# Mixing the expert weights of the last taps and of the third convolution on VectorE, from a layout by experts

## The chip, the core and the metric

The kernel runs on one core of one Trainium2 chip. The metric is the device time of one execution in microseconds (us). TensorE is written PE, VectorE DVE, ScalarE ACT, GpSimd POOL, SyncE SP; PEld is PE's loading of weights.

## The reference, cut to what matters

The program computes four layers on x of 4 images, 512 channels, 64x64, all in fp32. The change lies in layer 1, a conditional convolution: each image has its own weights, mixed from eight experts.

```python
def _L1_conv_ref(x, router_w, router_b, w1, w2, w3, g1, b1, m1, v1, ...):
    def _cond_conv(x, experts, rw, stride, padding):
        W = jnp.einsum('be,eoihw->boihw', rw, experts)          # one weight per image
        ...                                                      # convolution of each image with its W
    pooled = x.mean(axis=(2, 3))
    rw = jax.nn.sigmoid(pooled @ router_w.T + router_b)          # 8 numbers per image
    out = _cond_conv(x, w1, rw, 1, 0)                            # 1x1, 512 -> 128
    out = jax.nn.relu(_bn(out, g1, b1, m1, v1))
    out = _cond_conv(out, w2, rw, 1, 1)                          # 3x3, 128 -> 128
    out = jax.nn.relu(_bn(out, g2, b2, m2, v2))
    out = _cond_conv(out, w3, rw, 1, 0)                          # 1x1, 128 -> 512
    out = _bn(out, g3, b3, m3, v3)
    return jax.nn.relu(out + x)
```

Layer 0 is an attention over the 4096 positions with head size 64, layer 2 a linear attention with softplus features, layer 3 a projection with discounted cumulative sums along rows and columns and a gate.

## The kernel before

The images are worked through one after the other; for each of them `layer0` to `layer3` run in this order, and `xs` holds the image as four tiles of 128 partitions x 4 x 1024 ("pairs" of two blocks of 512 positions). PE's order is the order of the program over the whole kernel (`manual_schedule` with PE). DVE's order is the program's in the blocks of code that say so (the tail of `layer0`, the start of `layer2` and two parts after it, `layer3`). Elsewhere a scheduler places the instructions of DVE, ACT, POOL and SP.

**The weights of layer 1** are 17 pieces of 128 x 128: pieces 0 to 3 are the first convolution (`conv1`, one piece per 128 input channels), 4 to 12 the nine taps of the second, 13 to 16 the third (`conv3`). The mixed pieces stand in `wc`, the first 17 slices of the tile `wcq`. Each image loads the experts anew in five loads by SP: `ex0` (pieces 0-3), `ex4` (4-6), `ex7` (7-9), `ex10` (10-12), `ex13` (13-16). They go into buffers that are free at the time: `ex4`, `ex10`, `ex13` in the pool `bigp` (three buffers), `ex7` in `xpool`, `ex0` in `wlate`.

**Mixing on PE (`mix`, L170).** The DRAM tensor `packed` has on each partition one of four experts and one of 32 input channels: partition (e, i), then piece, quarter q of the input channels, half g of the experts, output channel. `sel` is 128 x 2 x 32: rw of the expert where the partition's i is the column's i, else zero. A matmul with `sel[:, g, :]` as weights sums four experts for 32 input channels; eight matmuls (two g, four q, each q in its own 32 columns of the array) give n pieces in one PSUM bank, and ACT copies them into `wc` (L178).

**Around it.** At the end of `layer0` (from L352, DVE in the program's order) the last pair's attention is normalised, rw is formed on DVE (L363 to L366), and from it `own` (L368), `part` (L371) and `sel` (L374). PE's order there is: two products of the output projection (`y`, L291), logit, another `y`, `mix` of `ex0`, the last `y`; then in `layer1` `mix` of `ex4` and `ex7`, `conv1(0)`, `mix` of `ex10`, `conv1(1)`, `conv1(2)`, `mix` of `ex13`, `conv1(3)`. After that comes `layer2`, which starts with the second and third convolutions: `conv2(0)`, `conv2(1)`, `conv3(0)`, `conv2(2)`, `conv3(1)` and so on.

The second convolution works on six sums of shifted rows instead of the rows themselves: `sums_of_six(pr)` (L430) forms them on DVE from `conv1`'s output of pair `pr`, twelve instructions of 128 x 256; `sums_of_taps` (L402) forms the matching sums of the nine taps on ACT and DVE, so it needs pieces 4 to 12 mixed. `conv2(pr)` (L459) has 36 matmuls less those at the edge; then ACT copies half of the result to `sp` (L472), DVE combines (`dq`, L473, to L480), ACT applies batch norm and relu (L484). `conv3` (L489) has two matmuls for each of four output blocks, and DVE adds the image (L495). In `layer2` DVE's order is written as `sums_of_six(0)`, `(1)`, `(2)`, the end of `conv2(0)`, `sums_of_six(3)`, the end of `conv2(1)`, the end of `conv3(0)`.

The PSUM tag `s` has three buffers of two banks (products `y`, `conv1`, `conv2`, `conv3` take them in turn), the tag `acc` two of one bank (`mix`, and the edge sums of `conv2`).

Of the kernel before, what the change touches and what calls it, by code (L numbers as in the profile page):

```python
# [8 lines left out]
F32 = mybir.dt.float32  # L9
AF = mybir.ActivationFunctionType  # L10
ALU = mybir.AluOpType
# [4 lines left out]
P = 128  # L16
# [4 lines left out]
KC = C // P  # L21
# [4 lines left out]
E = 8  # L26
# [19 lines left out]
def unshifted(ctx: ExitStack, tc: tile.TileContext, fits, x, wqkv_t, wout_t, router_t,  # L46
# [3 lines left out]
    nc = tc.nc  # L50
# [3 lines left out]
    bigp = ctx.enter_context(tc.tile_pool(name="bigp", bufs=3))  # L54
# [8 lines left out]
    def bank(name, shape=(P, NB)):  # L63
        return ps.tile(list(shape), F32, tag="acc", name=name)
# [16 lines left out]
    def load_pair(b, pr):  # L81

        t = xpool.tile([P, KC, 2 * NB], F32, tag="x", name=f"x_{b}_{pr}")
        src = x[b, :, pr * 2 * NB:(pr + 1) * 2 * NB].rearrange("(kc p) n -> p kc n", p=P)
        if b == 0 and pr == 0:
            for kc in range(KC):
                nc.sync.dma_start(t[:, kc, :], src[:, kc, :])
        else:
            nc.sync.dma_start(t, src)
        return t  # L90
# [4 lines left out]
    xs = [load_pair(0, pr) for pr in range(NPAIR)]  # L95
# [66 lines left out]
                             start=kc == 0, stop=kc == KC - 1)  # L162
        nc.vector.tensor_scalar(wr_sb, wo_t[:, 1, 0:E], col(SCALE), 1.0 / HW, ALU.mult, ALU.mult)

    def load_experts(b, j, n, pool, tag):
        ex = pool.tile([P, n, 4, 2, P], F32, tag=tag, name=f"ex_{b}_{j}")
        nc.sync.dma_start(ex, packed[:, j:j + n])
        return b, j, n, ex

    def mix(wc, sel, experts):  # L170

        b, j, n, ex = experts
        y = bank(f"mix_{b}_{j}", (P, n, P))
        for g in range(2):
            for q in range(4):
                nc.tensor.matmul(y[32 * q:32 * (q + 1)], sel[:, g, :], ex[:, :, q, g, :], start=g == 0, stop=g == 1,  # L176
                                 tile_position=(0, 32 * q))
        nc.scalar.copy(wc[:, j:j + n, :], y)  # L178

    def layer0(b, xs):  # L180


        tc.keep_in_program_order(nc.scalar.preload_act_table_set("natural_log_exp_and_others"))
        ex0 = load_experts(b, 0, KC, wlate, "late")
        key = bigp.tile([P, HW], F32, tag="big", name=f"key_{b}")
        qv = bigp.tile([P, 2, NPAIR * NB], F32, tag="big", name=f"qv_{b}")
# [95 lines left out]
        def sum_range(pr):  # L282
            i = b * NPAIR + pr
            nc.vector.tensor_reduce(stat[:, 0, i:i + 1], recs[pr], AX.X, ALU.add)
            nc.vector.tensor_reduce(stat[:, 1, i:i + 1], recs[pr], AX.X, ALU.min)
# [58 lines left out]

        pr = NPAIR - 1
        ex4 = load_experts(b, 4, 3, bigp, "big")
        for i in groups[-1]:
            values(i)
        ex7 = load_experts(b, 7, 3, xpool, "x")
        wcq = bigp.tile([P, NPIECE + 1 + 4 * NPAIR, P], F32, tag="big", name=f"wc_{b}")  # L350
        ex10 = load_experts(b, 10, 3, bigp, "big")
        with tc.manual_schedule(engines={mybir.EngineType.DVE}):  # L352
            sums(pr, early=False)
            for m in range(KC):
# [7 lines left out]
            rw = small.tile([P, E], F32, tag="rw", name=f"rw_{b}")  # L362
# [9 lines left out]
            sel = small.tile([P, 2, 32], F32, tag="sel", name=f"sel_{b}", bufs=1)  # L372
# [9 lines left out]
                xm = xs[pr - 1][:, m, :]  # L382
                nc.vector.tensor_tensor(xm, xm, flat(ring[8 + m]), ALU.add)
            sum_range(pr)
        return wcq, sel, ex4, ex7, ex10

    def layer1(b, xs, wcq, sel, ex4, ex7, ex10):
        wc = wcq[:, 0:NPIECE, :]
        qs = wcq[:, NPIECE + 1:, :].rearrange("p (a j) c -> p a (j c)", a=NPAIR)

        mix(wc, sel, ex4)
        mix(wc, sel, ex7)

# [6 lines left out]
        def sums_of_taps():  # L402
            part = block(f"part_{b}", (P, 4, P))[:, 0:3, :]
            nc.scalar.activation(taps[:, 0], g0, AF.Copy, scale=0.25)
            for k, c0, c1 in ((1, -1 / 6, 1 / 6), (3, 1 / 24, -1 / 12)):
                c2 = -1 / 6 if k == 1 else 1 / 6
                nc.scalar.activation(part, g0, AF.Copy, scale=c0)
                nc.vector.scalar_tensor_tensor(part, g2, c2, part, ALU.mult, ALU.add)
                nc.vector.scalar_tensor_tensor(taps[:, k], g1, -c1, part, ALU.mult, ALU.add)
                nc.vector.scalar_tensor_tensor(taps[:, k + 1], g1, c1, part, ALU.mult, ALU.add)  # L410
# [6 lines left out]
        def conv1(pr):  # L417
            y = pair_psum(f"c1_{b}_{pr}")
            for h in range(2):
                for kc in range(KC):  # L420
                    nc.tensor.matmul(y[:, h, :], wc[:, kc, :], xs[pr][:, kc, h * NB:(h + 1) * NB],  # L421
                                     start=kc == 0, stop=kc == KC - 1)
            rows = h1[:, :, 2 * pr * ROWS:2 * (pr + 1) * ROWS, :]
            yq = y.rearrange("p h (r q f) -> p f (h r) q", q=W // 4, f=4)
            for f in range(4):
                q = 1 if f == 0 else 0
                nc.scalar.activation(rows[:, f, :, q:q + W // 4], yq[:, (f - 1) % 4], AF.Relu,
                                     bias=bn_t[:, 0:1], scale=bn_s[:, 0:1])
# [67 lines left out]
                nc.scalar.activation(xm, xm, AF.Relu, bias=bn_t[:, 2 + m:3 + m])  # L496

        conv1(0)
        mix(wc, sel, ex10)
        sums_of_taps()  # L500
        conv1(1)
        ex13 = load_experts(b, 13, KC, bigp, "big")
        conv1(2)
        mix(wc, sel, ex13)
        conv1(3)
        return sums_of_six, conv2, conv3, wcq, qs

    def layer2(b, xs, sums_of_six, conv2, conv3, wcq, qs):

        ks = small.tile([P, NPAIR], F32, tag="ks", name=f"ks_{b}")  # L510
        g = bank(f"g_{b}", (P, C))
# [78 lines left out]
        with tc.manual_schedule(engines={mybir.EngineType.DVE}):  # L590
            sums_of_six(0)
            sums_of_six(1)
            sums_of_six(2)
            h2 = {0: conv2(0)}
            sums_of_six(3)
            h2[1] = conv2(1)
            conv3(0, h2[0])
# [288 lines left out]
    with tc.manual_schedule(engines={mybir.EngineType.PE}):  # L886
        for b in range(B):
            convs = layer1(b, xs, *layer0(b, xs))
            xs = layer3(b, xs, *layer2(b, xs, *convs))
# [395 lines left out]
@with_exitstack  # L1285
def tile_kernel(ctx: ExitStack, tc: tile.TileContext, *args):
    nc = tc.nc
    flagp = ctx.enter_context(tc.tile_pool(name="flagp", bufs=1))
    fits = flagp.tile([1, 2], mybir.dt.int32, tag="fits", name="fits")
    unshifted(tc, fits, *args)  # L1290

    n = nc.values_load(fits[0:1, 0:1], min_val=0, max_val=P)
    with tc.If(n < P):
        general(tc, *args)
# [50 lines left out]
```

## Time and profile before

| | |
|---|---|
| median of 3 runs | 2735.74 us (2735.30 to 2735.93) |
| the profiled execution's own time | 2737.18 us |
| its span, first to last instruction | 2735.4 us |
| mean granted PE clock | 0.998 |
| PE busy, share of the span | 2682.8 us, 98% |
| DVE busy | 1918.6 us, 70% |
| ACT busy | 1310.5 us, 48% |
| `mix` on PE, 12 mixes of three pieces (128x384) | 17.1 us in 192 records |
| `mix` on PE, 8 mixes of four pieces (128x512) | 15.4 us in 128 records |
| ACT's copies of mixed weights (L178) | 20, of 0.48 us (384) or 0.59 us (512) |
| loads of experts by SP | 12 of 1536 KB, 6.1 us to landing; 8 of 2048 KB, 7.6 us |

A page's line of a group gives the line of the kernel, the engine, the operation, out<-in by name and shape, the number of instructions, their busy time, the mean duration of one in ns, and the idle time of the engine just ahead of them with what ended it. In the chain of waits each row is a start, a duration and what ran; the chain is followed back from the last instruction to whatever released it. In the timeline each row is a start, a duration, the engine, and in brackets the idle time before it. PE's records show each fp32 matmul as two.

### The profile page before, as it was taken

Reading aid. Unit: us, or ns where it says so; the run is one execution under the profiler, and the core shown is the slowest. Engines: PE = TensorE matmul, PEld = TensorE weight load, DVE = VectorE, ACT = ScalarE, POOL = GpSimd, SP = SyncE. Lnnn points to the kernel's source line nnn. Section 1 sums busy time; section 2 is a strip of 40 time slices with the busy share of each in tenths; the row PEclk is TensorE's granted clock in tenths of the full one; section 3 lists DMA queues with packets and bytes.
Section 4 is the critical chain, followed back from the end, with each engine's and each line's share of the span. In section 5 each row is a group of like instructions: output and inputs, shape, how many; then the busy total and the mean of one; then the engine's idle time right before and its main releaser. Section 6 shows DMA issues by size and latency. Waiting matters only on the chain.

```text
span 2735.4 us, 25841 instructions
## 1 busy us (share of the span) xinstructions
PE 2682.8 (98%) x10174; PEld 1116.4 (41%) x10174; DVE 1918.6 (70%) x2133; ACT 1310.5 (48%) x1491; POOL 10.7 (0%) x26
## 2 busy tenths in 40 slices
PE   8999999999999999999999999999999999999998
PEld 3333364344333345444433334544443333454443
DVE  2688656787478766678747776667874787666787
ACT  4545344445554535345555553535554545352545
POOL 1000000000000000000000000000000000000000
PEclk9999999999999999999999999999999999999999
DMA  5000210021200021002220002101121000210011
GB/s 187 1 1 0 100 31 1 16 108 76 78 0 1 1 101 31 0 23 100 77 77 1 1 1 100 31 1 55 69 107 47 1 1 10 92 31 0 31 44 50
DMA packets 31986, 115.17 MB, mean 42 GB/s; under 512 B 2928, under 2 KB 12144, under 8 KB 29296
## 3 DMA queue, kind: packets, MB, share of 16 engines
q1 hardware_dynamic: 31856, 113.43, 11.0%
q8 instruction: 82, 1.34, 0.2%
q14 instruction: 48, 0.39, 0.0%
HBM read 79.86 MB, written 33.55 MB: 41 GB/s over the span
## 4 chain that ended last, share of the span: by engine, by line
PE 87%; DVE 8%; ACT 2%; issue 1%; DMA 1%; SPq 1%; DVEq 0%; ACTq 0%
PE s L237 17%; PE av L252 16%; PE sx L747 14%; PE zy L747 11%; PE kq L198 4%; PE c L421 4%; PE c L470 3%; PE c L493 2%; PE z L522 2%; PE vv L198 2%; PE wv L665 2%; PE g L584 2%; PE xtr L567 2%; PE y L291 2%; PE c2e L470 2%; PE mix L176 1%
## 5 line engine op out<-in xcount | busy, mean ns | idle before, releaser
L237 PE MATMUL s<-qv,key 64*128 64x512 f32 x2048 | 468.2, 602 | 1.8 <-ACT ring L240 1.8
L245 DVE TENSOR_TENSOR acc<-acc,ring 128x1024 f32<-128x1024 f32 x312 | 381.7, 1223 | 100.8 <-ACT ring L240 71.6
L240 ACT ACTIVATE ring<-s 128x1024 f32<-128x1024 f32 x336 | 317.7, 1039 | 223.6 <-PE s L237 223.6
L252 PE MATMUL av<-ring,qv 128*64 128x512 f32 x1344 | 304.5, 595 | 0.0
L237 PEld LDWEIGHTS s<-qv,key 64*128 64x128 f32 x2048 | 188.9, 187 | 274.3 <-issue 171.8
L245 DVE TENSOR_TENSOR acc<-acc,ringx 128x1024 f32<-128x1024 f32 x168 | 205.5, 1223 | 101.0 <-ACT ringx L240 88.2
L240 ACT ACTIVATE ringx<-s 128x1024 f32<-128x1024 f32 x176 | 172.1, 1040 | 206.0 <-PE s L237 206.0
L747 PE MATMUL sx<-t,sx 128*128 128x512 f32 x512 | 236.9, 597 | 0.0
L252 PEld LDWEIGHTS av<-ring,qv 128*64 128x64 f32 x1344 | 93.3, 137 | 198.6 <-issue 198.6
L252 PE MATMUL av<-ringx,qv 128*64 128x512 f32 x704 | 167.2, 598 | 0.0
L752 ACT COPY zy<-sx 128x512 f32<-128x512 f32 x64 | 36.5, 570 | 240.1 <-PE sx L747 230.6
L797 DVE TENSOR_TENSOR_SCAN t<-sx,t 128x512 f32<-128x512 f32 x128 | 148.8, 1210 | 1.7
L747 PEld LDWEIGHTS sx<-t,sx 128*128 128x128 f32 x512 | 95.9, 190 | 127.8 <-issue 121.1
L786 ACT COPY t<-s 128x1024 f32<-128x1024 f32 x64 | 127.1, 1993 | 40.5 <-DVE s L780 40.5
L756 ACT ACTIVATE e<-sx,prm_sb 128x512 f32<-128x512 f32 x128 | 87.0, 687 | 123.8 <-PE sx L747 123.8
L780 DVE TENSOR_TENSOR_SCAN s<-wc,s 128x512 f32<-128x512 f32 x128 | 146.0, 1204 | 0.0
L803 ACT ACTIVATE s<-t 128x1024 f32<-128x1024 f32 x64 | 125.5, 1987 | 1.0 <-DVE t L797 0.9
L747 PE MATMUL sx<-t,wq 128*128 128x512 f32 x256 | 117.0, 598 | 7.5 <-ACT e L756 7.5
L198 PE MATMUL kq<-x,wqkv_sb 128*64 128x512 f32 x512 | 117.0, 610 | 6.0 <-DMA x<-in_x_dram 6.0
L747 PE MATMUL zy<-t,wq 128*128 128x512 f32 x256 | 118.7, 604 | 2.5 <-ACT zy L752 2.5
L747 PE MATMUL zy<-x,wq 128*128 128x512 f32 x256 | 116.2, 594 | 0.0
L747 PE MATMUL sx<-x,wq 128*128 128x512 f32 x256 | 116.2, 594 | 0.0
(193 smaller groups left out, 3368.4 us busy)
## 6 DMA issues: line engine op xcount, KB each, us to landing
out_dram<-s SPq DMA_DIRECT2D x64, 512.0 KB, 2.6
x<-in_x_dram SPq DMA_DIRECT2D x15, 2048.0 KB, 8.3
ex<-in_packed_dram SPq DMA_DIRECT2D x12, 1536.0 KB, 6.1
ex<-in_packed_dram SPq DMA_DIRECT2D x8, 2048.0 KB, 7.6
wq<-in_wproj_t_dram SPq DMA_DIRECT2D x32, 256.0 KB, 5.1
x<-in_x_dram SPq DMA_DIRECT2D x4, 512.0 KB, 6.6
wv_sb<-in_wv_t_dram SPq DMA_DIRECT2D x1, 1024.0 KB, 11.4
wqkv_sb<-in_wqkv_t_dram SPq DMA_DIRECT2D x1, 384.0 KB, 3.1
```

Of the source, the lines that this page charges most:

```text
L198: nc.tensor.matmul(y[h * D:(h + 1) * D, :], wqkv_sb[:, kc, col0:col0 + D], xs[pr][:, kc, h * NB:(h + 1) * NB], start=kc == 0, stop=kc == K ...
L237: nc.tensor.matmul(s[:, h, :], key[r, kt * P:(kt + 1) * P], qry[r, pr * NB:(pr + 1) * NB], start=True, stop=True)
L240: nc.scalar.activation(p, s, AF.Exp)
L245: nc.vector.tensor_tensor(accs[pr], accs[pr], p, ALU.add)
L252: nc.tensor.matmul(avs[pr][h * D:(h + 1) * D, :], vt[:, kt, :], ring[i % RING][:, h, :], start=kt == 0, stop=kt == NT - 1)
L421: nc.tensor.matmul(y[:, h, :], wc[:, kc, :], xs[pr][:, kc, h * NB:(h + 1) * NB], start=kc == 0, stop=kc == KC - 1)
L470: nc.tensor.matmul(y[:, lo - a:hi - a], u, v[:, lo:hi], start=dy == 1, stop=dy == 2)
L747: nc.tensor.matmul(y, w[:, c, self.kind, self.j * P:(self.j + 1) * P], v[:, c, :], start=c == 0 and k in (1, 5), stop=c == 1, skip_group_c ...
L780: nc.vector.tensor_tensor_scan(self.half(i, h), along[:, self.j + 2 * i, :], self.half(i, h), 0.0, ALU.mult, ALU.add)
L786: nc.scalar.copy(self.t[i].rearrange("p (w r) -> p w r", w=W), self.s[i].rearrange("p (r w) -> p w r", w=W))
L797: nc.vector.tensor_tensor_scan(th, down[:, i, :], th, 0.0, ALU.mult, ALU.add)
L803: nc.scalar.activation(self.s[i].rearrange("p (r w) -> p w r", w=W), tw, AF.Sigmoid)
```

## The change

Two of the five mixes, of `ex10` (the last three taps) and of `ex13` (the third convolution), are done on DVE. Their experts are loaded from the DRAM tensor `experts`, which has for each piece and input channel (a partition) the eight experts' 128 outputs one after the other; so a partition's data of one piece is a run of 4 KB, where `packed` had one run of 12 or 16 KB for all pieces of the load. `mix_by_expert` multiplies the first expert's slice by rw's first column, and adds the seven others with a multiply and add each. rw is handed on to `layer1`. The mix of `ex10` is written at the start of `layer1`, that of `ex13` in `layer2` after `sums_of_six(2)`, ahead of `conv2(0)`. The three mixes of pieces 0 to 9 stay as they were.

```diff
--- before.py
+++ after.py
@@ -162,10 +162,21 @@
                              start=kc == 0, stop=kc == KC - 1)
         nc.vector.tensor_scalar(wr_sb, wo_t[:, 1, 0:E], col(SCALE), 1.0 / HW, ALU.mult, ALU.mult)
 
-    def load_experts(b, j, n, pool, tag):
-        ex = pool.tile([P, n, 4, 2, P], F32, tag=tag, name=f"ex_{b}_{j}")
-        nc.sync.dma_start(ex, packed[:, j:j + n])
+    def load_experts(b, j, n, pool, tag, pack=True):
+        if pack:
+            ex = pool.tile([P, n, 4, 2, P], F32, tag=tag, name=f"ex_{b}_{j}")
+            nc.sync.dma_start(ex, packed[:, j:j + n])
+        else:
+            ex = pool.tile([P, n, E, P], F32, tag=tag, name=f"ex_{b}_{j}")
+            nc.sync.dma_start(ex, experts[j:j + n].rearrange("n p e c -> p n e c"))
         return b, j, n, ex
+
+    def mix_by_expert(wc, rw, experts):
+        _, j, n, ex = experts
+        to = wc[:, j:j + n, :]
+        nc.vector.tensor_scalar(to, ex[:, :, 0, :], rw[:, 0:1], None, ALU.mult)
+        for e in range(1, E):
+            nc.vector.scalar_tensor_tensor(to, ex[:, :, e, :], rw[:, e:e + 1], to, ALU.mult, ALU.add)
 
     def mix(wc, sel, experts):
 
@@ -348,7 +359,7 @@
             values(i)
         ex7 = load_experts(b, 7, 3, xpool, "x")
         wcq = bigp.tile([P, NPIECE + 1 + 4 * NPAIR, P], F32, tag="big", name=f"wc_{b}")
-        ex10 = load_experts(b, 10, 3, bigp, "big")
+        ex10 = load_experts(b, 10, 3, bigp, "big", pack=False)
         with tc.manual_schedule(engines={mybir.EngineType.DVE}):
             sums(pr, early=False)
             for m in range(KC):
@@ -382,14 +393,15 @@
                 xm = xs[pr - 1][:, m, :]
                 nc.vector.tensor_tensor(xm, xm, flat(ring[8 + m]), ALU.add)
             sum_range(pr)
-        return wcq, sel, ex4, ex7, ex10
-
-    def layer1(b, xs, wcq, sel, ex4, ex7, ex10):
+        return wcq, sel, rw, ex4, ex7, ex10
+
+    def layer1(b, xs, wcq, sel, rw, ex4, ex7, ex10):
         wc = wcq[:, 0:NPIECE, :]
         qs = wcq[:, NPIECE + 1:, :].rearrange("p (a j) c -> p a (j c)", a=NPAIR)
 
         mix(wc, sel, ex4)
         mix(wc, sel, ex7)
+        mix_by_expert(wc, rw, ex10)
 
 
 
@@ -496,16 +508,14 @@
                 nc.scalar.activation(xm, xm, AF.Relu, bias=bn_t[:, 2 + m:3 + m])
 
         conv1(0)
-        mix(wc, sel, ex10)
         sums_of_taps()
         conv1(1)
-        ex13 = load_experts(b, 13, KC, bigp, "big")
+        ex13 = load_experts(b, 13, KC, bigp, "big", pack=False)
         conv1(2)
-        mix(wc, sel, ex13)
         conv1(3)
-        return sums_of_six, conv2, conv3, wcq, qs
-
-    def layer2(b, xs, sums_of_six, conv2, conv3, wcq, qs):
+        return sums_of_six, lambda: mix_by_expert(wc, rw, ex13), conv2, conv3, wcq, qs
+
+    def layer2(b, xs, sums_of_six, mix_last, conv2, conv3, wcq, qs):
 
         ks = small.tile([P, NPAIR], F32, tag="ks", name=f"ks_{b}")
         g = bank(f"g_{b}", (P, C))
@@ -591,6 +601,7 @@
             sums_of_six(0)
             sums_of_six(1)
             sums_of_six(2)
+            mix_last()
             h2 = {0: conv2(0)}
             sums_of_six(3)
             h2[1] = conv2(1)
```

## The prediction

> **What bounds the kernel now.** I read the busy shares first, then the shares of the chain that ended last, then that chain in order of time over one image's tail of layer 0 and layer 1 (300 to 362 us, first image), then VectorE (DVE) over the same stretch. From the page:
>
> ```profile
> PE 2682.8 (98%) x10174; PEld 1116.4 (41%) x10174; DVE 1918.6 (70%) x2133; ACT 1310.5 (48%) x1491; POOL 10.7 (0%) x26
> ...
> PE 87%; DVE 8%; ACT 2%; issue 1%; DMA 1%; SPq 1%; DVEq 0%; ACTq 0%
> ```
>
> TensorE (PE) is busy for 98% of the span and holds 87% of the chain: what leaves PE's queue is time, and so is what makes PE wait. The chain in order of time (start, us, what):
>
> ```profile
> 306.53 0.18 DVE own L368
> ...
> 306.73 0.17 DVE part L371
> ...
> 306.93 0.25 DVE sel L374
> ...
> 307.22 1.92 PE mix L176 x16
> 309.14 1.06 PE y L291 x4
> 310.20 2.72 PE mix L176 x32
> 312.92 7.07 PE c L421 x16
> 319.99 1.43 PE mix L176 x16
> 321.41 13.93 PE c L421 x32
> 335.34 1.85 PE mix L176 x16
> 337.20 7.07 PE c L421 x16
> 344.26 5.07 PE c L470 x24
> ```
>
> Three readings. The mixing of pieces 10-12 (319.99) and 13-16 (335.34) stands on the chain with conv1 (L421) before and after it. Two conv1 without a mix between them (321.41) take 13.93 us. And own, part, sel lie on the chain just before PE's first mix: PE stands still there. DVE over the stretch (start, us, ..., idle before it and who ended it):
>
> ```profile
> 317.12 0.68 DVE L285 TENSOR_REDUCE stat<-rec 128x1 f32<-128x512 f32 x1
> 321.99 0.76 DVE L440 SCALAR_TENSOR_TENSOR t<-h 128x256 f32<-128x256 f32 x2 [4.19 <-ACT h L427]
> ...
> 341.53 0.42 DVE L440 SCALAR_TENSOR_TENSOR wl<-t,t 128x256 f32<-128x256 f32 x1
> 349.99 0.69 DVE L473 TENSOR_TENSOR dq<-c,sp 128x512 f32<-128x512 f32 x1 [8.04 <-ACT sp L472]
> ```
>
> DVE has two holes here, 4.19 and 8.04 us; the other images show 4.18, 4.18, 3.60 and 8.04 each.
>
> [...] L533 takes 691 ns at N=1024, L726 with two tensors 1222. [...] the trace has no load of experts in 4 KB runs, only loads of x in such runs (2048 KB in 8.3 us, against 7.6 for experts of the same size in 16 KB runs).
>
> **The change, part by part.** The instruction order of both kernels, compared engine by engine, differs only in what follows.
>
> *PE, removed.* Two mixes of eight matmuls per image. A further conv1 in a row costs 13.93 - 7.07 = 6.86 us, and the last one 344.26 - 337.20 = 7.06 up to conv2. From the first conv1 to conv2 it was 344.26 - 312.92 = 31.34; without mixes it is 3 x 6.86 + 7.06 = 27.64. **Saved: 3.70 us per image, 14.8 in four** (the other images have the same distances to 0.01 us). ACT loses two copies (0.48 and 0.58 us), off the chain.
>
> *DVE, added.* Eight dependent instructions per mix. The nearest rows:
>
> ```profile
> L533 DVE TENSOR_SCALAR sp<-sp 128x1024 f32<-128x1024 f32 x16 | 11.1, 691 | 52.3 <-ACT sp L532 52.3
> ...
> L409 DVE SCALAR_TENSOR_TENSOR wl<-wc,part 128x384 f32<-128x384 f32 x8 | 4.4, 552 | 0.0
> ...
> L656 DVE SCALAR_TENSOR_TENSOR kv<-bv_sb,ksum,gk 128x512 f32<-128x512 f32 x4 | 3.0, 748 | 1.0 <-PE gk L655 1.0
> ```
>
> A scalar read per partition costs some 60 ns more (L808 750 against L769 689). So a step is 0.61 us at 384 elements and 0.75 at 512. The first multiply[...] is an estimate of 0.36 + 0.06 = 0.42 and 0.42 + 0.06 = 0.48 (0.61 and 0.75 if not). A dependent instruction starts 0.03 us after the end of the one that it reads (L448 at 338.14, after 337.35 + 0.76). Mix of 10-12: 0.42 + 0.03 + 7 x 0.64 = 4.9 us. Mix of 13-16: 0.48 + 0.03 + 7 x 0.78 = 6.0 us. Together 11 us an image, 44 on DVE; what matters is where.
>
> *In front of sel.* The scheduler put the first two steps of the mix of 10-12 ahead of sel: the multiply between own and part, the first add between part and sel. PE's mix of 0-3 waits for sel, and all of PE's queue behind it. With the multiply at 306.73, the add starts at 306.73 + 0.42 + 0.03 = 307.18, and sel, not dependent on it, some 0.08 before its end (four L296 of 1.28 us take 4.85), at 307.71 in place of 306.93: 0.78. If the multiply needn't wait for own (0.1 earlier), 0.68. I take **0.75 us per image, 3.0 in four**. Bounds: 0.55 (no surcharge for the scalar) and 1.0[...]; never a gain[...].
>
> *The wait that comes with it.* The multiply waits for the load of pieces 10-12. Behind it stand part, sel and four L296, and so PE. In SP's queue this load is second of three: issued at 294.76, 6.1 us to landing, thus at 300.9, 5.8 us before DVE asks. Its 128 packets of 12 KB become 384 of 4 KB: I take 0.1 to 0.6 us more ([...]8.3 against 7.6 scaled to 1.5 MB). The next load (pieces 7-9, landed at 305.5, used after 311) may come as much later. Cost nothing, covered by 5 us.
>
> *The other six steps of 10-12* come after L285: 6 x 0.64 = 3.8 us, in the 4.19 hole. L285 ends at 317.8 + 0.75, the steps at 322.4. The hole's end moves with conv1 to 321.99 + 0.75 = 322.7. Fits by 0.3 us; the last image, with its hole of 3.60, misses by 0.3, which the next hole (2.26 us before 337.35, about 1.3 after the change) takes up.
>
> *Load of 13-16.* SP now waits for DVE's last step (322.4) rather than PE's mix (issued at 321.5 before). Landing 7.6 us later, at 330; DVE asks at 341. Behind it in SP's queue are only the projection's weights, at 388.8. Nothing.
>
> *mix_last*, 6.0 us, goes into the 8.04 hole. conv1 now starts at 312.92 + 0.75 = 313.67 and conv2 at 341.3, 2.95 earlier. The sums of six of the third pair follow the third conv1: it ended at 321.41 + 13.93 = 335.3 and will end at 313.67 + 3 x 6.86 = 334.25, so those sums end 1.0 earlier, at 340.9, and mix_last at 346.9. L473 could start 2.95 earlier, at 347.0. **It fits with next to nothing to spare.** Behind it is some cover: conv3's fourth product needs the PSUM buffer that the first L495 frees. Before, that was freed at 362.97 and wanted at 364.6, so about 1.6 us of overflow cost nothing. Pieces 13-16 are first wanted by conv3, 10 us later still.
>
> *Sum.* 14.8 - 3.0 = 11.8 us. Against the profiled execution's own 2737.2 (span 2735.4, 1.8 around it) that is 2725.4; against the median of the runs shown, 2735.74, 1.4 lower, **2724.0**. Layers 2 and 3 and the next image's loads are released by PE's and DVE's progress, and the images follow each other at an even 677 us, so nothing swallows the shift. Some 0.2%, 5.5 us, is what a measurement of this kernel can tell from no change.
>
> **Rivals.**
> 1. *DVE overflows.* If a step took 1.2 us (the slices of the experts reading slower than rows), mix_last would take 9.6, overflow 3.5, pay 3.5 - 1.6 = 1.9; before sel the delay would be about 1.5: gain 3.7 - 3.4 = 0.3 an image, about 2734.5. For it: a fit with no reserve. [...]
> 2. *The load is late and DVE stands before sel*: the change ends **slower**. The place is the multiply between own and part. It costs PE one for one once the load takes more than 306.7 - 294.8 = 11.9 us, eats the gain at 11.9 + 2.95 = 14.9 us, and is slower by 0.2% past 16.2. At three times the present time to landing, 18.3 us: 6.4 - 2.95 = 3.45 an image lost, 2749.5. For it: a new layout with three times the packets. Against it: loads of x with such packets bring 2 MB in 8.3 us.
> 3. *Sel isn't held up.* If the two steps cost PE nothing, 14.8 us are gained: 2721. Against it: sel is on the chain.
> That the change doesn't do what it says is excluded: the order shows 16 matmuls per image gone from PE and 16 DVE instructions added.
>
> **How the numbers follow.** Forecast (sel's delay 0.55 to 1.0: 2723.1 to 2725.0; with an overflow of mix_last paid by up to 1 us an image, to 2729): 0.80. Rival 3: 0.04. Rival 1 and milder forms that leave under 5.5 us: 0.10. Rival 2: 0.06. So faster 0.84, same 0.10, slower 0.06. Range 2720.5 to 2731.
>
> **What would show it.** Right: no mix between conv1s, conv1 to conv2 in 27.6 us; DVE's multiply after own without a wait for a DMA; PE's wait before the first mix longer by 0.7; L473 still waiting for ACT's sp, or for mix_last by tenths. Wrong: a DMA as the releaser of the multiply, PE idle before conv2 or conv3, or steps well over 0.75 us.

## The result and the profile after

The changed kernel takes 2726.99 us, the median of 6 runs (2726.01 to 2728.76), against 2735.84 us of the kernel before on the same chip (6 runs, 2735.30 to 2738.34): a ratio of 0.9966, with a 95% interval of 0.9953 to 0.9979. A second set gave 2725.57 against 2736.25, 0.9961 (0.9948 to 0.9975). The profiled execution took 2727.02 us with a span of 2725.2, where that of before took 2737.18 with 2735.4.

The busy shares and the shares of the chain that ended last, after the change:

```profile
PE 2668.1 (98%) x10046; PEld 1112.3 (41%) x10046; DVE 1960.1 (72%) x2197; ACT 1306.8 (48%) x1483; POOL 10.8 (0%) x26
...
PE 86%; DVE 8%; ACT 3%; DMA 1%; issue 1%; SPq 1%; DVEq 0%; ACTq 0%
```

PE lost 14.7 us of work and DVE gained 41.5. PE still bounds. The chain in order of time, first image (start, us, what):

```profile
306.97 0.17 DVE own L379
307.14 0.52 DVE wc L177
...
307.73 0.59 DVE wc L179
308.32 0.16 DVE sel L385
...
308.52 1.92 PE mix L187 x16
...
314.22 27.66 PE c L433 x64
341.89 5.07 PE c L482 x24
```

The four `conv1` run as one piece of 27.66 us with no mix in it. From the start of the first `conv1` record to that of `conv2`'s it was 31.25 us in every image and is now 27.57: **3.68 us less in each** (the chain's rows, with other ends, give 31.34 and 27.67). The other half of the change is at the top: between `own` and `sel` stand two instructions of the mix (`wc`, L177 and L179), and they are on the chain. From `own`'s start to PE's first mix it was 0.69 us and is now 1.55 in every image: **0.86 us more**.

From `own` to layer 2's first product, a stretch that holds every changed instruction of PE and DVE, an image takes 79.34 us in place of 82.16: 2.82 less in each of the four, which is 3.68 - 0.86. On balance nothing else in it gained or lost.

DVE's timeline over the same stretch (start, us, ..., and in brackets the idle time before and what ended it):

```profile
307.06 0.60 DVE L177 TENSOR_SCALAR wc<-ex,rw 128x384 f32<-128x384 f32 x1
...
318.43 0.68 DVE L296 TENSOR_REDUCE stat<-rec 128x1 f32<-128x512 f32 x1
319.02 3.88 DVE L179 SCALAR_TENSOR_TENSOR wc<-ex,rw,wc 128x384 f32<-128x384 f32 x6
323.29 0.76 DVE L452 SCALAR_TENSOR_TENSOR t<-h 128x256 f32<-128x256 f32 x2 [0.39 <-ACT h L439]
...
342.07 5.48 DVE L179 SCALAR_TENSOR_TENSOR wc<-ex,rw,wc 128x512 f32<-128x512 f32 x7
347.62 0.69 DVE L485 TENSOR_TENSOR dq<-c,sp 128x512 f32<-128x512 f32 x1
```

The hole of 4.19 us before `t` now holds six steps and 0.39 us are left. The hole of 8.04 before `dq` (L485, before L473) holds the whole mix of pieces 13 to 16, and 0.07 us are left between the last step's end and `dq`. So `dq` is not late: it starts 5.73 us after `conv2` (344.26 and 349.99 before, 341.89 and 347.62 now). Counted from the start of `conv1` it came at 349.99 - 312.92 = 37.07 us before and comes at 347.62 - 314.22 = 33.40 now, 3.67 earlier, as much as PE gained.

What a step takes, from the groups by form (count, then busy us, mean ns of one, and the idle time before):

```profile
L179 DVE SCALAR_TENSOR_TENSOR wc<-ex,rw,wc 128x512 f32<-128x512 f32 x28 | 21.1, 752 | 1.0
...
L179 DVE SCALAR_TENSOR_TENSOR wc<-ex,rw,wc 128x384 f32<-128x384 f32 x28 | 17.3, 617 | 0.6
...
L177 DVE TENSOR_SCALAR wc<-ex,rw 128x384 f32<-128x384 f32 x4 | 2.4, 606 | 0.0
...
L177 DVE TENSOR_SCALAR wc<-ex,rw 128x512 f32<-128x512 f32 x4 | 1.9, 481 | 0.0
```

The multiply-and-adds are as priced. The first multiplies are odd: 384 elements take longer than 512.

**Where the time went.** Four images times (3.68 - 0.86) are 11.3 us. The profiled spans differ by 10.2. Of the 1.1 between them, 0.44 lie before the first image's `own`, which comes at 306.97 in place of 306.53: between 60 and 70 us the granted clock was 0.66 in this execution and 0.83 in that of before, and other executions show either. In the thirteen traces of this document the first `own` comes at 304.2 to 308.3 us, though up to there the kernels differ at most in how a load is laid out; so single executions differ by up to 4 us before the change begins. Another 0.42 are the sum of small differences in the three stretches from layer 2's features to the next image's `own` (594.3 to 595.6 us each, before 594.7 to 594.9), and 0.26 lie behind the last image's. The third of those stretches is 595.0 to 596.0 us in all twelve traces of changed kernels and 594.8 in the one trace of before; whether the change has a part in that is open. The changed places are the same in all images to 0.05 us.

### The profile page after: what moved, and what is told of

The parts are those of the page before. It is cut to its first block, busy times and chain, and to the rows that moved or that the text cites. A ratio compares the mean times of both kernels' runs of the same rounds, so it can differ in the third digit from the quotient of the medians.

```text
span 2725.2 us, 25637 instructions
## 1 busy us (share of the span) xinstructions
PE 2668.1 (98%) x10046; PEld 1112.3 (41%) x10046; DVE 1960.1 (72%) x2197; ACT 1306.8 (48%) x1483; POOL 10.8 (0%) x26
## 4 chain that ended last, share of the span: by engine, by line
PE 86%; DVE 8%; ACT 3%; DMA 1%; issue 1%; SPq 1%; DVEq 0%; ACTq 0%
PE s L248 17%; PE av L263 17%; PE sx L758 14%; PE zy L758 11%; PE c L433 4%; PE kq L209 4%; PE c L482 3%; PE z L532 2%; PE c L505 2%; PE wv L676 2%; PE vv L209 2%; PE g L594 2%; PE xtr L577 2%; PE y L302 2%; PE c2e L482 2%
```

## The experiments

**The changed kernel again**, beside the next three.

> The changed kernel itself, beside the next three on one chip, so that they can be set against it. If the working of the prediction holds with sel's delay as traced (0.86 us an image in place of 0.75), it is 4 x (3.68 - 0.86) = 11.3 us below before; if the six runs shown are typical, 8.9 below.

Measured: 2725.57 us, ratio 0.9961 (0.9948 to 0.9975), 10.7 less than before. So the 8.9 of the first set and the 11.3 of the trace are within what sets of runs differ by.

**The mix of 10 to 12 behind sel.** In `e1_sel_first` all eight steps are written after the last instructions of `layer0`'s DVE block; everything else is as changed.

```diff
             sum_range(pr)
+            mix_by_expert(wcq, rw, ex10)
         return wcq, sel, rw, ex4, ex7, ex10
...
-        mix_by_expert(wc, rw, ex10)
```

> The mix of pieces 10-12 is written on DVE after sum_range, so that all its eight steps come behind sel and the four additions to x. Theory (two steps stand before sel and hold PE up): own to PE's first mix falls back from 1.55 to 0.69 us, 0.86 x 4 = 3.4 us are gained on the changed kernel, about 14.7 below before. The eight steps (0.60 + 0.03 + 7 x 0.64 = 5.1 us) then run over the hole after the statistics by some 0.9 us, which the next hole (1.8 us in the changed kernel) takes up. Rival A (the delay before sel is hidden by something else on PE, or what DVE does later sets the pace): no gain, or up to 3 us lost, because the sums of six come 0.9 us later and mix_last has no reserve.

Measured: 2722.03 us, ratio 0.9948 (0.9935 to 0.9962), 14.2 less than before, 3.5 less than the changed kernel beside it. The chain in order of time:

```profile
304.24 0.18 DVE own L379
...
304.64 0.25 DVE sel L385
...
304.93 1.92 PE mix L187 x16
...
310.63 27.66 PE c L433 x64
```

`own` to PE's mix is 0.69 us again, as before the change, and the four `conv1` still take 27.66. All of the 0.86 us came back: 4 x 0.86 = 3.4, measured 3.5. The eight steps overrun the hole a little (the next instruction of DVE started without a wait, and the hole before the third pair's sums was 0.68 us in place of 1.80), and PE doesn't notice. **This version beats both kernels.**

**Each half alone.** `e2_last_only` leaves 10 to 12 on PE, `e3_taps_only` leaves 13 to 16 there.

```diff
--- e2_last_only against the changed kernel
-        ex10 = load_experts(b, 10, 3, bigp, "big", pack=False)
+        ex10 = load_experts(b, 10, 3, bigp, "big")
...
-        mix_by_expert(wc, rw, ex10)
...
         conv1(0)
+        mix(wc, sel, ex10)
--- e3_taps_only against the changed kernel
-        ex13 = load_experts(b, 13, KC, bigp, "big", pack=False)
+        ex13 = load_experts(b, 13, KC, bigp, "big")
         conv1(2)
+        mix(wc, sel, ex13)
         conv1(3)
-        return sums_of_six, lambda: mix_by_expert(wc, rw, ex13), conv2, conv3, wcq, qs
+        return sums_of_six, lambda: None, conv2, conv3, wcq, qs
```

> Only pieces 13-16 are mixed on DVE; 10-12 stay on PE from the packed layout. Theory: PE loses one mix with its changeovers, (335.34 + 1.85 + ...) i.e. 15.79 - 13.72 = 2.07 us an image, and sel isn't held up: 8.3 us below before, near 3 us above the changed kernel at most. If mix_last cost something by overflowing its hole, less: down to 4 below before.

> Only pieces 10-12 are mixed on DVE; 13-16 stay on PE from the packed layout. Theory: PE loses 1.63 us an image and pays 0.86 before sel: 0.77 x 4 = 3.1 us below before. Rival A (the delay before sel costs nothing): 6.5 below. Rival B (this half brings no gain at all): the same as before.

Measured: `e2_last_only` 2728.12 us, ratio 0.9969 (0.9957 to 0.9981), 8.1 less than before; `e3_taps_only` 2733.61, ratio 0.9991 (0.9983 to 1.0000), 2.6 less. The chain of the first, then of the second:

```profile
318.85 1.43 PE mix L187 x16
320.28 20.80 PE c L432 x48
341.08 5.07 PE c L481 x24
```

```profile
313.14 20.80 PE c L433 x48
333.94 1.85 PE mix L187 x16
335.79 7.07 PE c L433 x16
```

In each, one mix stands between `conv1`s and the other is gone. `conv1` to `conv2` is 29.20 us with 13 to 16 moved (2.05 less) and 29.62 with 10 to 12 moved (1.63 less). Only the second pays at `sel`: 1.55 from `own` to the mix, where the first has 0.69. So the halves are worth 4 x 2.05 = 8.2 and 4 x (1.63 - 0.86) = 3.1 by the traces, measured 8.1 and 2.6, and they add up to the 11.3 of both. The second gain is too small for its time alone to tell it from none (the interval ends at 1.0000); the trace, with the same distances in all four images, shows it.

**Why the first multiply is slow.** In `e4_even_halves` the multiply of three pieces reads and writes 64 outputs of all three pieces, then the other 64: the outermost dimension is two on both sides.

```diff
-        nc.vector.tensor_scalar(to, ex[:, :, 0, :], rw[:, 0:1], None, ALU.mult)
+        half = lambda t: t.rearrange("p n (h c) -> p h n c", h=2)
+        nc.vector.tensor_scalar(half(to), half(ex[:, :, 0, :]), rw[:, 0:1], None, ALU.mult)
```

> The changed kernel, with only the first multiply of each mix seen as two halves of 64 outputs (two times n times 64) on both sides. In the changed kernel that multiply took 0.60 us for three pieces[...] and 0.48 for four[...]. Theory: [...]the multiply of 10-12 takes 0.42 us, own to sel falls from 1.26 to about 1.08, and the whole gains 0.7 us, too little to be seen in a time. Rival: three pieces are slow for another reason (the stride between the slices, the scalar per partition): 0.60 stays.

Measured, in the one execution that was taken: 2723.56 us, span 2721.8. DVE's timeline:

```profile
304.23 0.41 DVE L178 TENSOR_SCALAR wc<-ex,rw 128x384 f32<-128x384 f32 x1
```

The multiply takes 0.41 us in place of 0.60, and `own` to PE's mix 1.36 in place of 1.55: the 0.19 us come through to PE one for one. It is the shape, then, not the type, the scalar or the place: three slices 1024 elements apart into one run of 384 took 0.60 us, the same slices as two halves on both sides 0.41, and from a source that is one run 0.42 (`e5_runs_of_512B`, next). What in the shape makes the difference, no run shows.

**Small runs, and the load that DVE waits for.** In `e5_runs_of_512B` the experts of 10 to 12 and 13 to 16 lie in memory by expert first, loaded piece by piece in runs of 512 bytes; the multiply's source is one run. The third piece's load comes behind that of pieces 7 to 9.

```diff
-            ex = pool.tile([P, n, E, P], F32, tag=tag, name=f"ex_{b}_{j}")
-            nc.sync.dma_start(ex, experts[j:j + n].rearrange("n p e c -> p n e c"))
+            ex = pool.tile([P, E, n, P], F32, tag=tag, name=f"ex_{b}_{j}")
+            for m in range(n):
+                nc.sync.dma_start(ex[:, :, m, :], experts[j + m])
...
-        nc.vector.tensor_scalar(to, ex[:, :, 0, :], rw[:, 0:1], None, ALU.mult)
+        nc.vector.tensor_scalar(to, ex[:, 0, :, :], rw[:, 0:1], None, ALU.mult)
...
-            nc.vector.scalar_tensor_tensor(to, ex[:, :, e, :], rw[:, e:e + 1], to, ALU.mult, ALU.add)
+            nc.vector.scalar_tensor_tensor(to, ex[:, e, :, :], rw[:, e:e + 1], to, ALU.mult, ALU.add)
```

> The changed kernel, with the experts of a mix loaded piece by piece (three or four loads) into a tile ordered by expert, then piece: runs of 512 B instead of 4 KB, and SP issues the third load of 10-12 behind that of 7-9. This presses on the wait before sel (the prediction's second rival). The source of the multiply is one run of 384, so it should take 0.42 us. Theory: three loads of 1.5 MB are issued from 291 on; at the 0.41 MB/us of the trace[...] the last lands near 306, DVE asks at 307: no or little wait, the same time as the changed kernel within 1 us. Rival: runs of 512 B take double the time: the multiply waits for a DMA by 1.5 us or more an image and the time is 6 us or more above the changed kernel.

Measured: 2731.14 us (20 runs), ratio 0.9982 (0.9975 to 0.9989), 5.6 above the changed kernel in `e0_after_again`; the expected little or no wait was wrong. That the last load would land near 306 was the author's estimate; no trace before this run showed a load of experts in runs of 512 bytes. DVE's timeline, then PE's in the second image:

```profile
307.18 0.42 DVE L178 TENSOR_SCALAR wc<-ex,rw 128x384 f32<-128x384 f32 x1 [0.57 <-DMA ex<-in_experts_dram]
```

```profile
983.38 3.34 PE L188 MATMUL mix<-ex,sel 128*32 128x512 f32 x16 [2.42 <-DVE sel L386]
```

The first line shows rival 2 of the prediction happening: a DMA as the releaser of the multiply, and behind it `sel` and PE. In four images DVE waited 2.8 us for the load, and `own` to PE's mix came to 2.01, 2.56, 2.06 and 1.96 us, together 2.4 more than in the changed kernel. That is less than half of the 5.6. The rest is in the second line: the mix itself takes 3.34 us, where it takes 1.92 in the changed kernel. The same stretch in windows (us, busy time of PE, PEld, DVE, ACT, POOL, then granted clock, DMA share, GB/s):

```profile
983.00:985.00 2.00, 1.62 (x12) 0.59 (x16) 2.00 (x5) 0.00 (x0) 0.00 (x0) 0.69 0.00 0
985.00:987.00 2.00, 2.00 (x12) 0.34 (x4) 2.00 (x2) 0.17 (x1) 0.00 (x0) 0.50 0.00 0
```

The granted clock was 0.50 for 3.41 us (983.74 to 987.15), and the DMA share was 0.00. This happened in the second and third image, after PE had waited 2.42 and 1.93 us, and not in the first and fourth, after 1.88 and 1.83. It cost 1.6 us each, 3.2 together, and 2.4 + 3.2 = 5.6. That the sum meets the difference of the medians so exactly is luck: the profiled execution itself took 2732.59 us, 1.45 above the median.

**Does a wait of PE bring the half clock about?** The rival was that the loads in small runs did. Three kernels without such loads, made from `e1_sel_first`, put more work ahead of `sel`: the first two steps of the mix (`e8a_two_steps_first`), the same with two small multiplies more whose result is written over later (`e8b_two_steps_and_two_small`), and three steps (`e8c_three_steps_first`). The two last arguments of `mix_by_expert` are here the first step and the one behind the last.

```diff
--- e8b_two_steps_and_two_small against e1_sel_first (e8a without the loop, e8c with 3 for 2)
+            for i in range(2):
+                nc.vector.tensor_scalar(wcq[:, 10 + i, :], ex10[3][:, i, 1, :], rw[:, 1:2], None, ALU.mult)
+            mix_by_expert(wcq, rw, ex10, 0, 2)
...
-            mix_by_expert(wcq, rw, ex10)
+            mix_by_expert(wcq, rw, ex10, 2, E)
```

> e1_sel_first, with the first two steps of the mix of 10-12 put between own and part by hand. PE's idle time before its first mix was 0.56 us in before and e1_sel_first, 1.41 in the changed kernel, and 1.88 (clock kept), 1.93 and 2.42 (clock at half for some 3 us, in the second and third image) in e5_runs_of_512B. Here it should be 0.56 + 1.06 = 1.6 us. Theory (half clock only where PE stands still for about 1.9 us or more): the clock stays at 1.00, mix to conv1 5.63 us as ever, and the time lies 4 x 1.06 = 4.2 us above e1_sel_first. Rival (the half clock in e5 came from something else, its DMA traffic for one): the same here, so this run tells them apart only with the next two.

> As e8a_two_steps_first, with two small multiplies more ahead of the two steps (128 x 128 each, into slices that the mix overwrites), some 0.2 us each: PE stands still for about 2.0 us. Theory: in most images the clock goes to half after the wait, the first mix takes 3.3 us in place of 1.9, mix to conv1 7.2 in place of 5.63: some 4 x (0.4 + 1.6) = 8 us above e8a. Rival (traffic): 5.63 stays, 1.6 us above e8a.

> As e8a_two_steps_first, with three steps in front of part: PE stands still for 1.6 + 0.65 = 2.3 us. Theory: half clock in all four images, mix to conv1 7.2 us, 4 x (0.65 + 1.6) = 9 us above e8a and so about 1 below before. Rival (traffic): 2.6 us above e8a.

Measured: 2728.07 us, ratio 0.9971 (0.9961 to 0.9980); 2731.25, ratio 0.9984 (0.9978 to 0.9991); 2733.09, ratio 0.9988 (0.9981 to 0.9995). PE's timeline, of `e8b_two_steps_and_two_small` in the second and third image, and of `e8c_three_steps_first` in the second:

```profile
982.93 1.92 PE L188 MATMUL mix<-ex,sel 128*32 128x512 f32 x16 [2.13 <-DVE sel L389]
1657.57 3.39 PE L188 MATMUL mix<-ex,sel 128*32 128x512 f32 x16 [2.13 <-DVE sel L389]
```

```profile
985.21 3.37 PE L188 MATMUL mix<-ex,sel 128*32 128x512 f32 x16 [2.27 <-DVE sel L387]
```

The same wait of 2.13 us was followed by the full clock in one image and by half of it in the next. In the profiled executions of both kernels it was one image of four; in `e8a_two_steps_first`, with 1.61 us, none. With `e5_runs_of_512B` and the changed kernel: of ten waits up to 1.88 us none brought it on, of ten from 1.93 us four did. So it happens without small runs, and my expectation that it would hit most or all images was wrong.

The first, by its wait 4 x (1.61 - 0.56) = 4.2 us above `e1_sel_first`, measured 6.0 above it in another set of runs. In the two profiled executions 2.5 us of the difference lie ahead of the first `own` (306.73 against 304.24), where the kernels do the same. Within this set the times agree in size: from the first of the three kernels to the others the waits alone account for 4 x 0.52 = 2.1 and 4 x 0.66 = 2.6 us, and 3.2 and 5.0 were measured; the excess of 1.1 and 2.4 is 0.7 and 1.6 images an execution at 1.5 us.

**What picks the image.** The traces answer this, though no run was made for it. In each of the thirteen, all changes of the granted clock lie whole steps of 3.413 us apart. In `e8b_two_steps_and_two_small` they come at 9.25 us, then 60.45 (15 steps later), 67.28 (17), 1657.89 (483), 1661.30 (484) and 2719.43 (794). So the changes in these traces fit steps of this length, and each half clock at a mix lasted one step. It went with how little PE did within the step before, and so with how much of the wait fell into a single step:

| kernel, image | step, us | PE busy in it, us | clock in the next step |
|---|---|---|---|
| `e5_runs_of_512B`, second | 980.33 to 983.74 | 0.98 | 0.50 |
| `e8b_two_steps_and_two_small`, third | 1654.47 to 1657.89 | 1.29 | 0.50 |
| `e8c_three_steps_first`, second | 981.35 to 984.76 | 1.59 | 0.50 |
| `e5_runs_of_512B`, third | 1656.17 to 1659.58 | 1.79 | 0.50 |
| `e8a_two_steps_first`, second | 980.65 to 984.06 | 1.80 | 1.00 |
| `e8b_two_steps_and_two_small`, second | 978.63 to 982.05 | 2.17 | 1.00 |
| the same, next step | 982.05 to 985.46 | 2.53 | 1.00 |

In the third image of `e8b_two_steps_and_two_small` the whole wait lies in one step; in the second the border at 982.05 cuts it in two. Around the waits before the first mix in all thirteen traces (52 waits) these four are the steps with the least work of PE, and no other was followed by half the clock. Where the steps lie differs from execution to execution (the first change comes at 8.8 to 13.5 us), which is the chance in it. The border near 1.8 us is a reading of these waits and not exact: early in `e4_even_halves` a step with 1.73 us kept the full clock, and one with 1.92 lost it. The shortest wait that half the clock followed was 1.93 us (`e5_runs_of_512B`, third image), of which 1.6 fell into one step.

**The cover behind the mix of 13 to 16.** The prediction put it at 1.6 us: so much may `dq` come late before `conv3` makes PE wait. Both kernels do more steps of this mix than needed, whose result is then written over: two steps (`e6a_two_more_steps`, 1.3 us) or all eight (`e6b_mix_twice`, 6.0 us).

```diff
-        return sums_of_six, lambda: mix_by_expert(wc, rw, ex13), conv2, conv3, wcq, qs
+        def mix_last():
+            mix_by_expert(wc, rw, ex13, 8)     # 2 in e6a_two_more_steps
+            mix_by_expert(wc, rw, ex13)
+        return sums_of_six, mix_last, conv2, conv3, wcq, qs
```

> The changed kernel, with the multiply and the first add of the mix of 13-16 done twice: 1.3 us more on DVE per image right where the mix fits its hole with nothing to spare. Theory: the end of conv2(0) starts 1.3 us later, but PE's first victim, conv3's fourth product, has 1.6 us to spare: no change against the changed kernel (within 1 us). Rival (there is no cover): 1.3 x 4 = 5.2 us slower than the changed kernel.

> The changed kernel, with the whole mix of 13-16 done twice: 6.0 us more on DVE per image. Theory: 6.0 - 1.6 = 4.4 us an image reach PE as waits of conv3, 17 us in all, so 6 to 7 above before. If DVE were covered further (conv3(0) wanted h2 only later): less than 10 us above the changed kernel. If nothing were covered: 24 us above it.

Measured: 2725.53 us, ratio 0.9963 (0.9949 to 0.9977), the changed kernel's time; and 2744.85, ratio 1.0028 (1.0017 to 1.0038), slower than before. With 1.3 us more PE's `conv3` runs on without a gap (7.03 us for four products). With 6.0 more, PE's timeline shows gaps:

```profile
359.84 4.03 PE L505 MATMUL c<-h,wc 128*128 128x512 f32 x8 [1.26 <-ACT h L496]
364.45 1.96 PE L505 MATMUL c<-h,wc 128*128 128x512 f32 x4 [0.58 <-DVE sp L486]
367.81 1.98 PE L505 MATMUL c<-h,wc 128*128 128x512 f32 x4 [1.40 <-DVE x L507]
```

PE waits for `conv3`'s input `h` (L496), then for `sp` (L486) and, ahead of `conv3`'s fourth product, for `x` (L507, before L495), which frees its PSUM; the prediction had named the last alone. From `conv2` to the first product of layer 2's features the image takes 48.94 us in place of 44.59: 4.35 more, and 6.0 - 1.6 is 4.4. In four images that is 17.4; the two kernels, run side by side, differ by 19.3. In the profiled executions 3.5 us of the difference lie ahead of the first `own`. Counted from `conv1`, `dq` came 1.16 us later than in the changed kernel with two steps more, at no cost, and 5.87 later with eight, at a cost of 4.35: so the cover is 5.87 - 4.35 = 1.5 us.

## Why the prediction was right, and where it was off

**PE's saving: right.** 3.70 us an image were predicted, 3.68 measured, in each image, and each half alone adds up to it.

**In front of sel: right in kind, off in size.** The two steps did stand on the chain, and what came ahead of `sel` cost PE one for one (`e1_sel_first` gets it all back). The term said 0.75 us, and it was 0.86. Two choices in it failed, with opposite signs. The multiply didn't wait for `own`: it starts at 307.06, `own` ends at 307.14. For that case the prediction had 0.68. And the multiply took 0.60 us and not 0.42. The 0.42 was an estimate; the trace of before supports it this far: L533, one tensor and an immediate scalar, took 691 ns at 1024 elements, as long as two tensors at half of that (L769, 689 at 512). By that, 384 elements would cost as much as 192 with two tensors, 0.36 us (an estimate from 552 ns at 384, L409, and 421 at 256, L440), and 0.06 more for the scalar. For four slices it held (0.48 predicted, 0.481 measured), for three it failed: they took the price of the other steps, 0.61 in the prediction. 0.68 + 0.18 = 0.86. The delay was within the bounds (0.55 to 1.0), and the sum becomes 11.3 in place of 11.8.

**The total: right in sign and size.** 2724.0 was predicted; the two sets gave 2726.99 and 2725.57. The first set lies outside the 2723.1 to 2725.0 that went with sel's delay alone, and within the range. Of the 3.0 us between forecast and the first, 0.5 are the two terms above; the rest is of the size of what executions differ by outside the change, as the granted clock between 60 and 70 us (0.66 or 0.83).

**DVE's steps: right.** 0.61 and 0.75 us predicted, 0.617 and 0.752 measured. The six steps fit the first hole (0.3 to spare predicted, 0.39 measured). In the last image, where the prediction saw them overrun by 0.3, 0.36 us were left: the five small instructions that shorten its hole to 3.60 us run between the steps, which take 3.91 us there and 3.88 in the first image. The mix of 13 to 16 fits the second with 0.07 to spare, as said, and the cover behind it is 1.5 us, where 1.6 were predicted. Rival 1, an overflow by slower slices, had no ground: a step on slices took 752 ns at 512 elements, where L656 of before took 748 on rows.

**The load: the conclusion right, the price not settled.** 0.1 to 0.6 us more were predicted for runs of 4 KB; the 0.1 was the author's estimate and rests on no trace. Measured from issue to landing: 8.4, 7.0, 6.5 and 6.4 us, where it was 6.1, 6.5, 6.1 and 6.1: 0.2 to 2.3 more. In `e0_after_again`, the same kernel, it was 6.4, 7.1, 6.4 and 6.3, which is 0.2 to 0.6 more, as predicted; and in `e2_last_only`, where these pieces came in runs of 12 KB, 6.3 to 7.7. So the 8.4 is not the layout's price, and what delayed that load is open. In the first image, issued at 295.20, it landed at 303.6, 3.5 us before DVE asked. Not the 5 us of the prediction, but enough. Of pieces 13 to 16 the load was issued at 322.93, landed 8.1 us later, and was asked for at 341.5.

**Rival 2, the late load: didn't happen, and was priced too low.** `e5_runs_of_512B` brought it about. "One for one" from the landing on held only for the wait itself; behind two of its four waits of PE (2.42 and 1.93 us) came half the clock for 3.41 us on top, which more than doubled the cost there. The changed kernel's wait of 1.41 us is 0.5 below the shortest that did so. Its second image had all of it in one step, with PE busy for 2.00 us, and kept the clock.

**Rival 3, sel not held up: wrong for the changed kernel.** It is what `e1_sel_first` attains by another order: 2721 was worked out, 2722.03 measured.

## What to carry to other kernels

Work that moves to an idle engine should be put into that engine's holes, and behind the instruction that the bounding engine waits for: ahead of it, it is paid one for one, and here that was 3.4 of 14.7 us, gained back by an order alone. Check a hole with what lies behind it: a move that filled a hole to the last tenth cost nothing here, 1.2 us more cost nothing either because 1.5 us of cover followed, and 5.9 us more cost 4.35 us an image. Where single executions differ by more than the change is worth, compare in the trace a stretch that holds the change alone, image by image. Before counting on the time that an operation takes elsewhere, measure it in the shape that it will have: the first multiply took 0.60 us on three slices, and 0.41 on the same slices as two halves.

## What the runs showed of the hardware

- A multiply by a per-partition scalar took 606 ns for three slices of 128 into one run, 481 for four slices (the changed kernel), and 410 for the same three slices taken as two halves (`e4_even_halves`) or 420 from one run (`e5_runs_of_512B`): less data can take longer.
- After a wait of PE of 1.93 us or more, in 4 cases of 10, the granted clock fell to 0.50 for 3.41 us, and the mix took 3.3 to 3.4 us in place of 1.92; after ten waits of 1.41 to 1.88 us it never did.
- All changes of the granted clock in an execution lay whole steps of 3.413 us apart. A wait before the mix was followed by half the clock where PE was busy for 0.98 to 1.79 us of a step, and by the full clock where it was 1.80 or more.
- The same 1.5 MB took 6.2 to 8.5 us from issue to landing in runs of 4 KB (ten traces) and 6.1 to 7.7 in runs of 12 KB (two traces): the scatter is larger than the difference.
